# One pair of tiles instead of two multiplied block by block, in a conditional layer with a LoRA feed-forward (fp32, one core)

## The chip, the cores and the metric

The kernel runs on one core of a Trainium2 chip. The metric is device time in microseconds of one execution. Before the change the median of three runs is 460.17 us (460.08 to 460.25).

## The reference

x has 64 batches of 64 channels of 1024 values, so 4096 rows (tokens) of 1024. Each batch picks one of 16 matrices of 64x64, the rows are mixed with it, and the result goes through a linear layer with a gated low-rank addition:

```
W = weights[condition]                                  # [64, 64, 64]
y = einsum('bct,bcd->bdt', x, W)
gate_logits = einsum('bsd,ed->bse', y, gate_w)          # 8 experts
weights, selected = top_k(gate_logits, 2);  weights = softmax(weights)
result = einsum('bsd,od->bso', y, base_w) + base_b      # 1024 -> 1024
low = einsum('bsd,erd->ebsr', y, lora_A)                # rank 16
lora_out = einsum('ebsr,eor,bse->bso', low, lora_B, w_full)
out = x + result + 2.0 * lora_out
```

## The kernel before, in words

**Tiles.** The 4096 rows are 32 tiles of 128, taken as 16 pairs. The mixing matrix acts on rows and the linear layer on columns, so the kernel multiplies x by the big matrix first (z = x B) and mixes rows of z afterwards. B has 1024 rows and 1160 columns: 128 of the low-rank part, 8 of the gate, 1024 of the base weights, padded to three column groups of W = 388 (the first uses 384). With four groups of 256 rows, B is a 4x3 matrix of blocks b11 to b43, and a pair of tiles is a 2x4 matrix of blocks a11 to a24.

**High and low halves.** Every operand is split in two parts, high and low, and each product of two operands takes three matmuls: high x high, high x low, low x high. `split_x` (L280) does it for x blocks and `split_w` (L328) for weight blocks: ScalarE casts the high part (`copy`, L234), VectorE subtracts it to get the low part (`sub`, L231). `zstep` (L407, matmuls at L414) issues the three matmuls for one half f of a block of 256 rows, so a block product is six matmuls.

**Two ways to multiply a pair.** The plain way multiplies all 2 x 4 x 3 = 24 block pairs: 144 matmuls (`plain`, L612). The other way is a bilinear scheme with 20 products p1 to p20 (`class Pair`), 120 matmuls. It needs sums of x blocks (`Operands`, VectorE at L292), sums of weight blocks (`SUMS` and `make`, VectorE at L342, each then split like a block), and additions of the products from PSUM into SBUF (`mix`, VectorE at L740; `keep` and `pass_on`, ScalarE at L234 and L723). The sums of weights are made once and serve every later pair.

NPLAIN = 2 says how many pairs go the plain way. The list PLAIN (L539) holds their block steps, the first pair's with the order of the weights' loading, the later ones tile after tile. ORDER (L549) holds the products of the remaining pairs: the first HEAD, then for each pair its TAIL (p14, p15, p2, p8, p9) interleaved with the HEAD of the next.

**After z.** `post` (L508) takes a column group of a tile: zh and zl are split from it, L447 multiplies by the tile's mixing matrix (bdh, bdl), `gate` (L472) takes two of eight experts with small VectorE and ScalarE operations (the last at L493), L500 transposes the gated low part, its halves lth and ltl are split and multiplied by lbh and lbl. `finish` (L452) copies the outcome to xtok with ScalarE for tiles of plain pairs; for the others VectorE adds it to xtok at L457. For plain pairs x and the bias are added afterwards by accumulating DMAs on POOL (`late_sum`), for the others they are loaded and accumulated beforehand (`load_tok`, SP and POOL).

**What sets the order.** The body does not issue instructions directly. It adds steps to a `Program` (L80), each with an engine, a cost, what it reads and writes, and a due time. `run` (L111) then plans the steps on a model of the engines and issues them in the planned order, the one with the least slack first. The due times come from PLAIN and ORDER, and `ends[NPLAIN]` is the due time by which the sums of weights in SUMS and LATER are planned:

```
        pr.horizon, h = ends[NPLAIN], pr.horizon
        make(SUMS.get(m, ""))
        pr.horizon = h
```

On the chip every engine runs its instructions strictly in the issued order and waits on semaphores for the others. Matmul accumulators are eight PSUM banks: z0 to z3 (called X, Y, R, Q in the products), a0, a1, o0, o1. A product that reuses a bank waits until the earlier sum has been read from it.

Of the kernel before, what the change touches and what calls it, by code (L numbers as in the profile page):

```python
# [34 lines left out]
OUTS = ((NG, N0, 0), (0, W, N0 - NG), (0, W, N0 - NG + W))  # L35
KQ = 4
NPAIR = NT // 2
NPLAIN = 2
TOP = 3.0e38
NWARM = 39  # L40

# [38 lines left out]
class Program:  # L80
# [7 lines left out]
    def add(self, engine, cost, fn, reads=(), writes=(), due=None, first=False, size=0.0, early=None, port=False,  # L88
            after=0.0):

        n = len(self.steps)
        engine, cost = (e if isinstance(e, (list, tuple)) else [e] for e in (engine, cost))
        deps = set()
        for b in list(reads) + list(writes):
            if b in self.writer:
                deps.add(self.writer[b])
        for b in writes:
            deps.update(self.readers.get(b, ()))  # L100
        for b in reads:
            self.readers.setdefault(b, []).append(n)
        for b in writes:
            self.writer[b], self.readers[b] = n, []
        deps.discard(n)
        self.steps.append(dict(eng=dict(zip(engine, cost)), fn=fn, deps=deps, first=first, size=size, port=port,
                               lag=FLIGHT + QUEUE + size * DMA if size else 0.0, after=after,
                               due=self.horizon if due is None else due,
                               early=SP in engine and not reads if early is None else early))
# [59 lines left out]
def cond_ffn_kernel(ctx, tc, xT, x, idx, cw, wall, bias, lb, out):  # L169
# [63 lines left out]
    def copy(e, o, a):  # L233
        (nc.scalar.copy if e == ACT else nc.vector.tensor_copy)(o, a)  # L234
# [93 lines left out]
    def split_w(m, p, step=2):  # L328

        b, h, l = raw[m], Block(f"wh_{m}_{p}", F32R), Block(f"wl_{m}_{p}", F32R)  # L330
        hi[p], lo[p] = h, l
        for j in range(0, 2, step):
            a = slice(j, j + step)
            add(ACT, 0.2 + 0.00083 * W * step, lambda e, a=a: copy(e, h.ap()[:, a], b.ap()[:, a]), b.keys[a], h.keys[a])
            add(DVE, tt_cost(W * step), lambda e, a=a: sub(e, l.ap()[:, a], b.ap()[:, a], h.ap()[:, a]),
                b.keys[a] + h.keys[a], l.keys[a], port=True)
# [27 lines left out]
    def make(text):  # L364
        for q in (t.split() for t in text.split("; ") if t):
            if q[0] == "-":
                drop(raw.pop(q[1]))
            elif q[1] == ">":
                split_w(q[0], q[2])
                drop(raw.pop(q[0]))  # L370
            else:
                mix_w(q[0], q[2], q[4], ALU.add if q[3] == "+" else ALU.subtract, q[6] if len(q) > 5 else None)
# [55 lines left out]
    def outs(c):  # L428

        c, p = c if isinstance(c, tuple) else (c, slice(0, CN[c]))  # L430
        lo, o, n = max(OUTS[c][0] - p.start, 0), OUTS[c][2] + max(p.start - OUTS[c][0], 0), p.stop - p.start
        return n, slice(lo, n), slice(o, o + n - lo), p
# [19 lines left out]
    def finish(i, c, b):  # L452
        (_, s, o, _), j = outs(c), i % 3
        if i < 2 * NPLAIN:
            return add(ACT, 0.2 + 0.00085 * (s.stop - s.start), lambda e: copy(e, xtok[j][:, o], bank[b][:, s]),
# [84 lines left out]
    PLAIN += [(i, 2, k) for i in range(2) for k in LASTK]  # L540
    for q in range(1, NPLAIN):
        PLAIN += [(i, c, k) for c in range(3) for i in (2 * q, 2 * q + 1) for k in range(KQ)]
    t = 4.9
    for i, c, k in PLAIN:
# [3 lines left out]
        ends_plain = t  # L548
    ORDER = [(NPLAIN, p) for p in HEAD]  # L549
    for q in range(NPLAIN, NPAIR):  # L550
        if q == NPAIR - 2:
# [17 lines left out]
    def load_split_w(m, **how):  # L569
        load_w(m)  # L570
        split_w(m, SINGLE.get(m, m), **how)
        pr.horizon, h = ends[NPLAIN], pr.horizon
        make(SUMS.get(m, ""))
# [38 lines left out]
    def plain(i, c, k):  # L612
        if (i, k) not in xa0:
            us = xrs.two()
            for d in range(2):
                load_x(i, k + d, us[d])
            xa0[i, k], xa0[i, k + 1] = split_x(us)
            xrs.give(*us)
        if (i, c) not in zb:
            zb[i, c] = f"z{take('z', 4)}"  # L620
            if c == 0 and i > 1:
                load_cond(i)
        ks, m = LASTK if c == 2 and i < 2 else range(KQ), f"b{k + 1}{c + 1}"
        for f in range(2):
            zstep(("plain", i, c, k, f), zb[i, c], xa0[i, k], SINGLE.get(m, m), f, k == ks[0] and f == 0,
                  k == ks[-1] and f == 1, CN[c])
        left[i, k] -= 1
        if not left[i, k]:
            xas.give(xa0[i, k])
        if k == ks[-1]:  # L630
            post(i, c, split_z(CN[c], lambda: bank[zb[i, c]][:, :CN[c]], zb[i, c]))
            if c == 2:
                late_sum(i)
                store(i, range(3))

    for i, c, k in PLAIN:
        pr.horizon = due["plain", i, c, k, 1] + LAG + 8.0
        plain(i, c, k)
    pr.horizon = ends[NPLAIN]
    for m in ("b11", "b21", "b12", "b22", "b13", "b23", "b43"):  # L640
# [223 lines left out]
```

## Time and profile before

| what | value |
|---|---|
| median of 3 runs | 460.17 us (460.08 to 460.25) |
| the profiled execution | 460.46 us |
| its span, first to last instruction | 458.7 us |
| mean granted TensorE clock | 1.000 |
| ScalarE busy (ACT) | 227.2 us (50%) |
| VectorE subtractions for the low parts of x (L231, 512 wide) | 130, 685 ns each |
| VectorE additions of products (L740, 388 wide) | 126 with one PSUM operand first, 558 ns each |
| DMA | 75.00 MB, mean 164 GB/s |

PE is TensorE's matmuls and PEld its weight loads, DVE is VectorE, ACT ScalarE, POOL GpSimd and SP the queue that issues most loads. A duration in the profile is that of one instruction from its start to its end; successive instructions of an engine can overlap, so where an engine is full the distance between starts is shorter than the duration. In the rows of 40 slices one slice is 11.5 us. The first matmul on data starts at 5.02 us, the last result is added at 454.1 us.

### The profile page before, as it was taken

How to read it: one execution, taken by the hardware profiler on the slowest of the kernel's cores; microseconds unless marked ns; L12 is line 12 of the kernel's file. 1: busy time of each engine (PE TensorE's matmuls, PEld its weight loads, DVE VectorE, ACT ScalarE, POOL GpSimd, SP SyncE). 2: the span in 40 equal slices, each digit the busy share in tenths (PEclk: the TensorE clock that was granted, in tenths of full speed). 3: DMA queues.
4: the chain of work that ended last, by engine and by line, in shares of the span. 5: the costliest groups of instructions: out<-in, count | busy, mean ns of one | idle time of the engine just before them, and what ended most of it. 6: DMA issues, size and time to landing. Idle time of an engine off the chain costs nothing.

```text
span 458.7 us, 7577 instructions
## 1 busy us (share of the span) xinstructions
PE 452.7 (99%) x2621; PEld 449.7 (98%) x2621; DVE 383.5 (84%) x941; ACT 227.2 (50%) x520; POOL 89.6 (20%) x107
## 2 busy tenths in 40 slices
PE   8999999999999999999999999999999999999995
PEld 8999999999999999999999999999999999999995
DVE  5999997879989788796987979789797988888674
ACT  5864666543736345373543646354454544546331
POOL 3030214121303021220303003030210403103000
PEclk9999999999999999999999999999999999999999
DMA  8932748977768462764847456565565746556142
GB/s 279 352 117 47 153 107 198 213 211 202 180 206 202 172 161 87 217 131 163 199 127 202 108 182 148 172 162 133 191 123 185 173 129 193 116 174 149 51 134 91
DMA packets 36229, 75.00 MB, mean 164 GB/s; under 512 B 4432, under 2 KB 22240, under 8 KB 36192
## 3 DMA queue, kind: packets, MB, share of 16 engines
q0 software_dynamic: 10560, 36.72, 33.5%
q1 hardware_dynamic: 25200, 37.32, 25.9%
q10 hardware_dynamic: 432, 0.49, 0.4%
q8 instruction: 20, 0.33, 0.3%
q14 instruction: 17, 0.14, 0.1%
HBM read 57.74 MB, written 16.78 MB: 162 GB/s over the span
## 4 chain that ended last, share of the span: by engine, by line
PE 97%; DMA 1%; DVE 1%; ACT 0%; issue 0%
PE ps_z L414 76%; PE ps_o L447 15%; PE ps_a L447 6%; DMA w_b<-in_w 1%; PE ps_a L500 1%; DVE wl_b_b L231 0%; DVE xtok L457 0%; DVE st L740 0%; ACT wh_b_b L234 0%; DVE xl L231 0%; PE ps_z L447 0%; DVE xh L234 0%
## 5 line engine op out<-in xcount | busy, mean ns | idle before, releaser
L231 DVE TENSOR_TENSOR xl<-xr,xh 128x512 fp32r<-128x512 f32 (+1 forms) x138 | 92.1, 670 | 20.0 <-ACT xh L234 19.8
L414 PE MATMUL ps_z<-wh_t_p,xh 128*128 128x388 f32 (+1 forms) x308 | 105.3, 342 | 0.1
L414 PE MATMUL ps_z<-wh_t_p,xl 128*128 128x388 f32 (+1 forms) x308 | 104.3, 339 | 0.0
L414 PE MATMUL ps_z<-wl_t_p,xh 128*128 128x388 f32 (+1 forms) x308 | 104.3, 339 | 0.0
L234 ACT CAST xh<-xr 128x512 fp32r<-128x512 f32 (+1 forms) x136 | 82.5, 610 | 37.2 <-PE ps_z L414 32.5
L740 DVE TENSOR_TENSOR st<-ps_z,st 128x388 f32<-128x388 f32 x126 | 70.2, 558 | 21.2 <-PE ps_z L414 20.2
L292 DVE TENSOR_TENSOR xr<-xr 128x256 f32<-128x256 f32 (+1 forms) x139 | 69.6, 526 | 3.6 <-DMA xr<-in_xT 3.4
L414 PE MATMUL ps_z<-wh_b_p,xh 128*128 128x388 f32 (+1 forms) x180 | 61.4, 341 | 0.0
L414 PE MATMUL ps_z<-wh_b_p,xl 128*128 128x388 f32 (+1 forms) x180 | 60.9, 338 | 0.0
L414 PE MATMUL ps_z<-wl_b_p,xh 128*128 128x388 f32 (+1 forms) x180 | 60.8, 338 | 0.0
L414 PEld LDWEIGHTS ps_z<-wh_t_p,xh 128*128 128x128 f32 x308 | 57.8, 188 | 1.2 <-DVE st L740 0.7
L414 PEld LDWEIGHTS ps_z<-wl_t_p,xh 128*128 128x128 f32 x308 | 57.9, 188 | 0.0
L414 PEld LDWEIGHTS ps_z<-wh_t_p,xl 128*128 128x128 f32 x308 | 57.9, 188 | 0.0
L464 POOL DMA_DIRECT2D out<-xtok x30 | 16.8, 560 | 193.6 <-DVE xtok L457 89.6
L234 ACT CAST zh<-st 128x388 fp32r<-128x388 f32 (+1 forms) x70 | 36.1, 517 | 22.1 <-DVE st L740 15.2
L381 POOL DMA_DIRECT2D xtok<-in_bias x28 | 27.0, 964 | 96.9 <-DMA xtok<-in_x 89.6
L394 POOL DMA_INDIRECT bdr<-in_cw,rows x32 | 36.9, 1155 | 26.4 <-DVE zl L231 17.7
L457 DVE TENSOR_TENSOR xtok<-ps_o,xtok 128x388 f32<-128x388 f32 (+1 forms) x56 | 30.9, 554 | 11.2 <-PE ps_o L447 10.7
L723 ACT ACTIVATE ps_z<-ps_z 128x388 f32<-128x388 f32 x42 | 20.1, 478 | 40.5 <-PE ps_z L414 39.4
L231 DVE TENSOR_TENSOR zl<-st,zh 128x388 fp32r<-128x388 f32 (+1 forms) x70 | 38.7, 554 | 0.9 <-ACT zh L234 0.6
L414 PEld LDWEIGHTS ps_z<-wh_b_p,xh 128*128 128x128 f32 x180 | 33.8, 188 | 0.2
L414 PEld LDWEIGHTS ps_z<-wl_b_p,xh 128*128 128x128 f32 x180 | 33.8, 188 | 0.0
(143 smaller groups left out, 873.0 us busy)
## 6 DMA issues: line engine op xcount, KB each, us to landing
xr<-in_xT SPq DMA_DIRECT2D x128, 128.0 KB, 3.2
xtok<-in_bias POOLq DMA_DIRECT2D x32, 512.0 KB, 7.1
out<-xtok POOLq DMA_DIRECT2D x30, 512.0 KB, 3.2
xtok<-in_x SPq DMA_DIRECT2D x28, 512.0 KB, 3.6
w_b<-in_w SPq DMA_DIRECT2D x10, 388.0 KB, 5.9
xtok<-in_x POOLq DMA_DIRECT2D x4, 512.0 KB, 6.6
out<-xtok SPq DMA_DIRECT2D x3, 194.0 KB, 2.2
bdr<-in_cw,rows POOLq DMA_INDIRECT x32, 5.3
```

The costliest lines, as they stand in the source:

```text
L231: eng[e].tensor_tensor(o, a, b.bitcast(F32), ALU.subtract)
L234: (nc.scalar.copy if e == ACT else nc.vector.tensor_copy)(o, a)
L292: add(DVE, tt_cost(2 * P * len(os)), lambda e: nc.vector.tensor_tensor(some(xr, os), some(xr, xs), some(xr, ys), f), [("xr", u) for u in s ...
L381: add(POOL, 1.1, lambda e: nc.gpsimd.dma_start(xtok[j], bias.broadcast_to([P, T]), accum_op=ALU.add), writes=keys, size=TWICE * 4.0 * T * P)
L394: add(POOL, 1.04, lambda e: nc.gpsimd.indirect_dma_start(out=bdr[j], out_offset=None, in_=cw, in_offset=bass.IndirectOffsetOnAxis(ap=rows[ ...
L414: nc.tensor.matmul(z, l[:, j, n], w.ap()[:, f, :cols], start=(start and q == 0), stop=(stop and q == 2), skip_group_check=True)
L447: nc.tensor.matmul(d, l, r, start=(start and m == 0), stop=(stop and m == len(mms) - 1), skip_group_check=True)
L457: add(DVE, 0.09 + 0.00104 * (s.stop - s.start), lambda e: nc.vector.tensor_tensor(xtok[j][:, o], bank[b][:, s], xtok[j][:, o], ALU.add), [ ...
L464: add(POOL, 1.0, lambda e: nc.gpsimd.dma_start(out[i * P:(i + 1) * P, o], xtok[j][:, o]), src, size=4.0 * P * (o.stop - o.start))
L500: add(PE, 0.107, lambda e: nc.tensor.matmul(tp, low[i % 2][:, :ER], ident, is_transpose=True, start=False, stop=False, skip_group_check=True),
L723: add(ACT, 0.2 + 0.00085 * W, lambda e: nc.scalar.mul(z[b], z[x], scale), [BANKS[x]], [BANKS[b]])
L740: add(DVE, 0.09 + 0.00104 * W, lambda e: nc.vector.tensor_tensor(unit(u), a(), b(), f), reads, [ukey(u)])
```

## The change

One constant is changed.

```diff
@@ -35,7 +35,7 @@
 OUTS = ((NG, N0, 0), (0, W, N0 - NG), (0, W, N0 - NG + W))
 KQ = 4
 NPAIR = NT // 2
-NPLAIN = 2
+NPLAIN = 1
 TOP = 3.0e38
 NWARM = 39
```

With it PLAIN holds the steps of pair 0 only, and ORDER begins with the twenty products of pair 1, whose x sums, additions of products and token loads go the way of the other pairs. The due time of the sums of weights, `ends[NPLAIN]`, becomes the end of pair 1's products instead of pair 2's. In `finish`, tiles 2 and 3 are added by VectorE instead of being copied by ScalarE. The planner plans all steps anew, so the order of instructions on every engine changes from the first microseconds on.

## The prediction

> **What bounds the kernel now.** I read the page's busy shares first, then busy time by stage, the chain that ended last, the waits, and the timeline of the first 75 us.
>
> ```profile
> PE 452.7 (99%) x2621; PEld 449.7 (98%) x2621; DVE 383.5 (84%) x941; ACT 227.2 (50%) x520; POOL 89.6 (20%) x107
> ...
> PE   8999999999999999999999999999999999999995
> ...
> DVE  5999997879989788796987979789797988888674
> ...
> PEclk9999999999999999999999999999999999999999
> ...
> PE 97%; DMA 1%; DVE 1%; ACT 0%; issue 0%
> ```
>
> Over the span TensorE is the bound: both its rows are full, the clock is whole, the chain is 97% matmuls. But VectorE's row stands at 9 in slices 2 to 6, so I cut the span by stage.
>
> ```profile
> core 0: us, PE busy (x) PEld busy (x) DVE busy (x) ACT busy (x) POOL busy (x), PEclk, DMA share, GB/s
> 9.00:75.00 66.00, 66.00 (x380) 65.56 (x379) 63.16 (x121) 43.51 (x90) 12.33 (x13) 1.00 0.60 168
> 75.00:102.00 27.00, 27.00 (x158) 26.96 (x157) 21.84 (x55) 13.65 (x33) 6.97 (x9) 1.00 0.87 201
> 102.00:129.00 27.00, 27.00 (x158) 26.92 (x157) 24.16 (x63) 13.14 (x31) 6.01 (x7) 1.00 0.77 205
> 129.00:156.00 27.00, 27.00 (x156) 26.93 (x156) 23.82 (x63) 12.90 (x32) 5.66 (x7) 1.00 0.62 184
> ```
>
> From 9 to 75 us two engines are full at once: TensorE 66.0 of 66, VectorE 63.2 of 66. VectorE splits the weights there and builds their sums. Afterwards it needs 21.8 to 24.2 us of each 27.0 (one pair of tiles, 158 matmuls). The only margin in the first stage is that the weight sums are wanted late:
>
> ```profile
> 72.81 0.96 DVE L231 TENSOR_TENSOR wl_g_p<-w_b,wh_g_p 128x776 fp32r<-128x776 f32 x1
> ...
> 96.64 0.33 PE L414 MATMUL ps_z<-wl_g_p,xh 128*128 128x388 f32 x1
> ```
>
> The last weight operand (wl_g, for p9) is ready at 73.8 and first used at 96.64: 22.8 us of lead. TensorE's waits hold 1.7 us on VectorE in all.
>
> **Matmuls removed.** The order in which the two programs queue their instructions differs by 24 matmuls, all 384 columns wide at L414. Consecutive starts of such matmuls are 0.175 us apart (10.23 to 10.40), so 24 x 0.175 = 4.2 us off TensorE. If TensorE stays the bound, all of it counts.
>
> Here a rule speaks for the change. The Trainium skill, Perfetto Trace Analysis, section Identifying the Most-Contended Engine, says to optimize the engine with the highest occupancy, TensorE judged by its weight-load share: 98% against VectorE's 84%. By it the sum is 460.46 - 4.2 = 456.3. The row of 9 to 75 us has the matmuls leave just where VectorE is at 96%, so the shares over the span don't settle it.
>
> **Work added to VectorE.** Counted in both orders, with the spacing of consecutive starts (776 wide 0.876, 512 0.603, 388 0.475, 256 0.335, 248 0.32): 15 more of 512 (9.0), 14 more of 388 (6.7), 2 more of 248 (0.6), 6 fewer of 256 (-2.0). That is 14.3 us more over the kernel. After 75 us VectorE has about 3 us to spare per pair, so there it costs nothing; before 75 us nothing hides it. ScalarE gains five 512-wide casts (0.62 each) and three copies (0.48) and loses three smaller ones, about 3 us; at 43.5 of 66 it has room, so I cost that at nothing. If ScalarE's queue failed to keep ahead, its casts would delay VectorE one for one, which the idle term below covers.
>
> **Weight sums moved.** All 20 products' weights are now wanted one pair earlier, so the 22.8 us lead meets a TensorE that arrives some 34 us sooner. VectorE queues its work in order, so I add up its queue in the changed program from the b21 split (9.04 us, the same place as before) to the wl_g split: 44 of 776 (38.5), 15 of 512 (9.0), 17 of 388 or 384 (8.1), 16 of 256 (5.4), 6 of 128 (1.2), lbl (1.14), small gate operations (2.1): 65.5 us, so wl_g is ready at 74.5 at the earliest. The same sum over the old queue gives 71.7 against 73.8 seen, so it errs low by about 2.
>
> TensorE, also in order, reaches the matmul reading wl_g after 309 matmuls from the one at 8.10. In the trace 508 matmuls from that one took 88.54 us (to 96.64), or 0.1743 each: 62.0. So it waits 74.5 - 62.0 = 12.5 us at least. Other points in the same two queues:
>
> The transpose of tile 1's gate wants L493's output at 34.9; the VectorE queue gives it at 40.3: 5.4 late. p18's xl half: wanted 46.4, ready 59.2: 12.8. p10 of the first product pair writes the bank that L740 must first read for c12: wanted 51.3, free 64.9: 13.6. p10 of the next pair: wanted 78.9 (406 matmuls), free 92.8: 13.9. Beyond that VectorE gains its 3 us per pair, and I count no more waits. These are waits of one in-order queue on another, so the largest counts, not their sum: 13.9 us if VectorE never idles.
>
> It idles some. A weight sum waits for nothing new, but behind L740, L486 and the ltl split (each waits for TensorE or ScalarE) the whole VectorE queue stands, the xl halves included, and TensorE stands for those. From both sides: 0 at least; at most 2.8, the idle time of the 9 to 75 row. I take 1.2, because 1.1 of that 2.8 was one wait at 73.8 to 74.9, by which time VectorE had caught up, and part lies ahead of work that nobody needed yet. Total wait 15.1.
>
> A second rule bears on the 65.5. The Trainium skill, VectorE: DVE Perf Modes, section The TRN2 errata, gives (N+151)/0.96 ns for an fp32 two-input operation: 966 for 776. The row shows 0.96 as duration, but starts 0.876 apart (12.43 and 13.31 for 776 wide): the end of one overlaps the next. Summing durations would add about 0.088 for each of the 92 large instructions, 8.1 us, and give some 479; I take the spacing.
>
> **Queues and loads.** The x tiles for the second pair's products are loaded by SP from about 20 us, ahead of and around b23; the row's DMA share of 0.60 and a landing time of 3.2 us leave room. POOL's accumulations for tile 2 move ahead of bdr loads needed only near 73 us. Nothing, at least nothing below zero since TensorE isn't fed sooner; at most one landing, 3.2, inside the range.
>
> **Sum.** Profiled execution 460.46 (span 458.7 and 1.8 around it) - 4.2 + 15.1 = 471.4. The median of the runs is 0.3 below that execution: 471.1.
>
> **Rivals.**
> First, the gain holds: faster, 460.17 - 4.2 = 456.0. Its one mechanism is that TensorE's wait stays below 4.2 us, because the sums needed for each product are always built ahead. It decides at p10: VectorE would have to deliver by 51.3 + 4.2 = 55.5 what its queue ends at 64.9, so 46.5 us for 55.9 us of work. For it: 22.8 us of lead, no wait over 0.4 us now. Against: the queue is in order and VectorE was full. 4%.
> Second, only the wl_g point binds (VectorE runs gapless and later banks come free sooner): 460.17 - 4.2 + 12.5 = 468.5. 18%.
> Third, hand-offs between the two engines add to the queue: both starved engines wait on each other at each of the c22, c12, c13 sums, the idle term is 2.8 and a load adds up to 3.2: 472.7 to about 476. 22%.
> My forecast, 469.5 to 472.7: 54%. The gain and the wait cancel (460): 2%; I know no reason for it but chance. That the change doesn't do what it says is excluded by the 24 matmuls counted.
>
> A measurement tells about 0.2% of this kernel from no change: faster 0.04, within 0.01, slower 0.95. The range takes in the second case and half of the third: 468.3 to 475.
>
> **What would show it.** TensorE idle of about 15 us between 34 and 95 us, put down to VectorE (first at the L500 transpose near 35 us, then xl and wl of the second pair, then L740); VectorE near 100% from 9 to 75; no new idle after 100 us; wl_g's split ending near 75 to 76. If TensorE's gaps are under 8 us or continue into every later pair, or if ScalarE or a DMA ends them, my sum is wrong.

## The result, and the profile after

The changed kernel takes 479.91 us (median of 479.85, 479.88, 479.95 and 485.0) against 460.21 for the kernel before beside it: a ratio of 1.0453, 95% interval 1.0402 to 1.0504. That is 19.7 us slower, 8.8 more than forecast, and above the range (468.3 to 475.0). The profiled execution is one of 479.85 us, with a span of 478.1.

The page of the changed kernel, same rows as before the change:

```profile
PE 455.2 (95%) x2597; PEld 446.7 (93%) x2597; DVE 398.1 (83%) x966; ACT 229.2 (48%) x525; POOL 87.8 (18%) x105
...
PE   8894989999999999999989999999999999999996
...
DVE  4899999998698878979877888988788897877675
...
PEclk9898899999999999999999999999999999999999
...
PE 80%; DVE 10%; DMA 7%; issue 2%; ACT 1%; POOL 0%; DVEq 0%; POOLq 0%; ACTq 0%
```

The counted edits are there: 24 matmuls fewer (2621 to 2597), and VectorE has 25 instructions and 14.6 us of busy time more (383.5 to 398.1; 14.3 was counted). What differs is the chain: TensorE's share has fallen from 97% to 80%, VectorE holds 10%, and DMA holds 7%, which no step of the prediction had. In TensorE's row, slices 2, 4 (36 to 48 us) and 6 are no longer full, nor is slice 21, near 245 us. Busy time by stage, in the stages used before:

```profile
core 0: us, PE busy (x) PEld busy (x) DVE busy (x) ACT busy (x) POOL busy (x), PEclk, DMA share, GB/s
9.00:75.00 66.00, 53.85 (x275) 50.30 (x274) 61.76 (x107) 38.84 (x75) 10.13 (x12) 0.92 0.65 179
75.00:102.00 27.00, 26.36 (x152) 25.75 (x151) 25.85 (x67) 12.35 (x32) 6.73 (x7) 1.00 0.55 164
102.00:129.00 27.00, 26.44 (x153) 26.06 (x152) 22.03 (x55) 12.61 (x31) 5.74 (x6) 1.00 0.65 169
129.00:156.00 27.00, 25.85 (x150) 25.44 (x149) 22.47 (x58) 12.30 (x30) 5.01 (x6) 1.00 0.51 139
```

From 9 to 75 us TensorE gets 275 matmuls through instead of 380. That was forecast in kind. Two things were not: VectorE is busy 61.8 of 66, so it idles for 4.2 us in a stage where I had allowed 1.2; and after 102 us, with VectorE at 22 of 27 and so with time to spare, TensorE still issues 149 to 152 weight loads where it issued 156 or 157. The waits of TensorE's weight loads over the whole kernel (us in total, times, longest):

```profile
PEld ps_z L414 <- DVE st L740: 6.5, 7, 2.1
PEld ps_z L414 <- DVE xl L231: 4.5, 4, 2.7
PEld ps_a L500 <- DVE low L493: 4.3, 1, 4.3
PEld ps_z L414 <- ACT xh L234: 2.8, 1, 2.8
```

Before, all waits on VectorE behind 5 us summed to 1.7 and none was on ScalarE. Beside VectorE's queue, which was forecast, two of these lines led to causes that were not.

**A wait on ScalarE, at 11 us.** The timelines of TensorE, ScalarE and VectorE of the changed kernel, in order of time (start, duration; the bracket is idle time before the instruction and what ended it):

```profile
12.42 0.30 ACT L234 CAST bdh<-bdr 128x128 fp32r<-128x128 f32 x1 [3.12 <-DMA bdr<-in_cw,rows]
...
12.75 0.29 DVE L231 TENSOR_TENSOR bdl<-bdr,bdh 128x128 fp32r<-128x128 f32 x1 [2.43 <-ACT bdh L234]
...
13.82 0.45 PE L414 MATMUL ps_z<-wh_b_b,xh 128*128 128x384 f32 x1 [2.47 <-ACT xh L234]
```

The replanned ScalarE queue has the cast of the first gathered mixing matrix (bdh) right behind the casts that start at 8.15 and 8.90. The gather was issued on POOL at 6.67 and has landed about 5.7 us later, so ScalarE stands still from 9.3 to 12.4, its next casts of weights and x stand behind it, VectorE behind those, and TensorE behind both. In the kernel before, the same cast lay eight casts further back, and found its data there:

```profile
15.12 0.29 ACT L234 CAST bdh<-bdr 128x128 fp32r<-128x128 f32 x1
```

**Waits on L740 behind a load.** 5.4 of the 6.5 us of the first line lie after 105 us (before: 0.7). One of them, in the timelines of POOL, SP, VectorE and TensorE:

```profile
233.90 1.03 POOL L381 DMA_DIRECT2D xtok<-in_bias  x1
...
234.47 0.33 SPq L380 DMA_DIRECT2D xtok<-in_x  x1
235.23 0.33 SPq L276 DMA_DIRECT2D xr<-in_xT  x1
...
241.57 0.69 DVE L292 TENSOR_TENSOR xr<-xr 128x512 f32<-128x512 f32 x1 [2.29 <-DMA xr<-in_xT]
...
243.00 0.55 DVE L740 TENSOR_TENSOR st<-ps_z,st 128x388 f32<-128x388 f32 x1
...
243.60 0.44 PE L414 MATMUL ps_z<-wh_h_p,xh 128*128 128x388 f32 x1 [1.77 <-DVE st L740]
```

An x load, issued just behind a bias accumulation and a token load, needs 6.3 us (235.23 to 241.57, when the instruction that waits for it starts) where the page's median is 3.0. VectorE's sum of x blocks (L292) waits for it at the head of the queue, the addition L740 that frees a PSUM bank stands behind it, and TensorE waits for the bank. L292 waits 10.1 us for x loads after 105 us, ten times. Before the change, in the same window:

```profile
DVE xr L292 <- DMA xr<-in_xT: 0.8, 2, 0.5
PEld ps_z L414 <- DVE st L740: 0.7, 2, 0.4
```

To place the loss I add up TensorE's lateness: the sum of what the distance between two successive matmul starts exceeds the usual one (0.176 us for 388 columns, 0.175 for 384, 0.115 for 248), from 5 us on. This is worked out from the timelines; the labels of the experiments stand in the section below.

| lateness of TensorE up to | 50 us | 103.5 us | 200 us | 440 us |
|---|---|---|---|---|
| before | 1.6 | 2.2 | 2.9 | 5.2 |
| after | 14.5 | 21.7 | 24.1 | 29.1 |
| bd | 12.6 | 19.1 | 21.6 | 25.2 |
| bdthinx | 12.0 | 17.7 | 19.1 | 22.0 |
| bdthinb | 11.2 | 17.3 | 18.2 | 20.6 |
| bdlo | 11.4 | 11.9 | 12.8 | 15.3 |
| bdlo2 | 11.5 | 15.6 | 17.3 | 27.7 |

After minus before is 19.5 us up to 103.5 us and 4.4 behind that. With the 4.2 us of matmuls that are gone, 23.9 - 4.2 = 19.7, against 19.4 between the two profiled executions.

### The profile page after: what moved, and what is told of

Read it like the earlier page. It is cut to its first block, busy times and chain, and to the rows that moved or that the text cites. A ratio compares the mean times of both kernels' runs of the same rounds, so it can differ in the third digit from the quotient of the medians.

```text
span 478.1 us, 7584 instructions
## 1 busy us (share of the span) xinstructions
PE 455.2 (95%) x2597; PEld 446.7 (93%) x2597; DVE 398.1 (83%) x966; ACT 229.2 (48%) x525; POOL 87.8 (18%) x105
## 4 chain that ended last, share of the span: by engine, by line
PE 80%; DVE 10%; DMA 7%; issue 2%; ACT 1%; POOL 0%; DVEq 0%; POOLq 0%; ACTq 0%
PE ps_z L414 61%; PE ps_o L447 13%; PE ps_a L447 5%; DMA xr<-in_xT 4%; DVE xl L231 2%; DVE xr L292 2%; DVE wl_t_p L231 1%; DVE st L740 1%; DMA bdr<-in_cw,rows 1%; DVE w_b L342 1%; DVE zl L231 1%; DMA idx_sb<-in_idx 1%; PE ps_a L500 1%; DVE xtok L457 1%; ACT xh L234 1%
## 5 line engine op out<-in xcount | busy, mean ns | idle before, releaser
L414 PE MATMUL ps_z<-wh_t_p,xh 128*128 128x388 f32 (+1 forms) x330 | 113.3, 343 | 1.6 <-ACT ps_z L723 1.4
L414 PE MATMUL ps_z<-wl_t_p,xh 128*128 128x388 f32 (+1 forms) x330 | 112.0, 339 | 0.8 <-DVE wl_t_p L231 0.8
L414 PE MATMUL ps_z<-wh_t_p,xl 128*128 128x388 f32 (+1 forms) x330 | 111.9, 339 | 0.5 <-DVE xl L231 0.5
L231 DVE TENSOR_TENSOR xl<-xr,xh 128x512 fp32r<-128x512 f32 (+1 forms) x143 | 95.7, 671 | 19.6 <-ACT xh L234 19.1
L740 DVE TENSOR_TENSOR st<-ps_z,st 128x388 f32<-128x388 f32 x135 | 75.0, 557 | 13.8 <-PE ps_z L414 13.0
L292 DVE TENSOR_TENSOR xr<-xr 128x512 f32<-128x512 f32 (+1 forms) x143 | 75.1, 543 | 11.0 <-DMA xr<-in_xT 10.7
L414 PEld LDWEIGHTS ps_z<-wh_t_p,xh 128*128 128x128 f32 x330 | 62.2, 188 | 3.9 <-ACT ps_z L723 2.1
L414 PEld LDWEIGHTS ps_z<-wl_t_p,xh 128*128 128x128 f32 x330 | 62.2, 189 | 1.1 <-DVE wl_t_p L231 1.1
L414 PEld LDWEIGHTS ps_z<-wh_t_p,xl 128*128 128x128 f32 x330 | 62.2, 188 | 1.1 <-DVE xl L231 1.1
L381 POOL DMA_DIRECT2D xtok<-in_bias x30 | 28.4, 947 | 79.2 <-DMA xtok<-in_x 70.4
L234 ACT CAST bdh<-bdr 128x128 fp32r<-128x128 f32 x32 | 9.5, 300 | 61.0 <-PE ps_o L447 57.9
```

Of the source, the lines that this page charges most:

```text
L231: eng[e].tensor_tensor(o, a, b.bitcast(F32), ALU.subtract)
L292: add(DVE, tt_cost(2 * P * len(os)), lambda e: nc.vector.tensor_tensor(some(xr, os), some(xr, xs), some(xr, ys), f), [("xr", u) for u in s ...
L381: add(POOL, 1.1, lambda e: nc.gpsimd.dma_start(xtok[j], bias.broadcast_to([P, T]), accum_op=ALU.add), writes=keys, size=TWICE * 4.0 * T * P)
L414: nc.tensor.matmul(z, l[:, j, n], w.ap()[:, f, :cols], start=(start and q == 0), stop=(stop and q == 2), skip_group_check=True)
L740: add(DVE, 0.09 + 0.00104 * W, lambda e: nc.vector.tensor_tensor(unit(u), a(), b(), f), reads, [ukey(u)])
```

## The experiments

The theory after the result: three waits, one behind the other. VectorE's queue up to the last weight sum (the forecast, some 15 us), the gather's cast in ScalarE's queue (some 3 to 4), and x loads that land late after 100 us (some 4 to 5). Rivals: the whole loss is VectorE's queue, and the other two waits hide in it; or TensorE's clock, which fell to 0.5 of full speed behind the long waits, is part of it.

**bd: the changed kernel, with the gather's cast planned no earlier than 16 us.**

```diff
-        add(ACT, 0.28, lambda e: copy(e, bdh[j], bdr[j]), [("bdr", j)], [("bdh", j)])
+        add(ACT, 0.28, lambda e: copy(e, bdh[j], bdr[j]), [("bdr", j)], [("bdh", j)], after=16.0)
```

> The changed kernel with one thing put back: ScalarE's cast of the first two gathered mixing matrices (bdh) may be planned no earlier than 16 us, so that it no longer stands in ScalarE's queue ahead of the casts of b22 and of x blocks while its gather is still on its way. Theory of an early queue block (3.1 us of ScalarE waiting for the gather, passed on to VectorE and from there through its full queue to every later product): 476.3 to 477 us, 3 to 3.6 below the changed kernel's 479.9. Rival, that VectorE's later backlog hides that wait (largest wait counts, not the sum): 479 to 480, no change.

Measured: 476.11 us, ratio 1.0342 (1.0325 to 1.036): 3.8 us less than the changed kernel. The cast now starts at 16.82 without a wait. So the standstill was not hidden behind VectorE's shortage: it comes first in time, and all three engines stand in it. By the lateness, 2.6 of it come back before 103.5 us and 1.3 behind it, where the new plan of the whole kernel also lies a little otherwise. All further experiments but n3 start from bd.

**bdlo: bd, and the low halves of the last ten weight sums are not computed** (their matmuls read the high half instead; that part of the products is left out).

```diff
+HALF = ("p10", "p4", "p13", "p7", "p17", "p3", "p15", "p14", "p8", "p9")
...
-        b, h, l = raw[m], Block(f"wh_{m}_{p}", F32R), Block(f"wl_{m}_{p}", F32R)
+        b, h = raw[m], Block(f"wh_{m}_{p}", F32R)
+        l = h if p in HALF else Block(f"wl_{m}_{p}", F32R)
...
+            if l is h:
+                continue
```

> As bd, and VectorE no longer computes the low halves of ten weight sums (those of p10, p4, p13, p7, p17, p3, p15, p14, p8, p9): the matmuls that read them read the high half instead, so the number of matmuls is the same and that part of the result is left out. It takes 10 x 0.876 = 8.8 us out of VectorE's queue before 80 us. Theory that VectorE's queue of weight work sets the first 75 us: 7 to 9 us below bd, about 468. Rival, that hand-offs and a lowered TensorE clock set it: under 3 us below bd.

Measured: 466.15, ratio 1.0125 (1.0108 to 1.0142): 10.0 us less than bd for ten instructions of 0.876 us, 8.8 us of VectorE's queue. By the lateness 7.2 come back up to 103.5 us (19.1 to 11.9) and 2.7 later. 6.0 of the 7.2 lie between 50 and 103.5 us. bd by stage, with the columns as above:

```profile
50.00:75.00 25.00, 22.46 (x120) 20.58 (x119) 24.07 (x46) 14.89 (x31) 4.94 (x6) 1.00 0.76 192
```

and bdlo:

```profile
50.00:75.00 25.00, 25.00 (x144) 24.97 (x143) 23.84 (x60) 17.31 (x38) 6.39 (x7) 1.00 0.75 200
75.00:102.00 27.00, 27.00 (x158) 26.93 (x157) 24.26 (x62) 12.06 (x29) 5.89 (x7) 1.00 0.66 183
```

VectorE is about as full as in bd, but finishes the sums sooner, and TensorE is full again from 50 us on. So VectorE's queue sets the stretch from 50 us to its last weight sum. Ahead of 50 us bdlo gives nothing back: its lateness there is 11.4, bdthinb, which keeps all the sums, has 11.2, and the two first long waits are as in bd (4.5 us at the transpose of tile 1, 2.4 at the xl half behind it). What puts these down to VectorE's queue is bd's trace:

```profile
30.00:41.00 11.00, 6.59 (x38) 6.03 (x37) 11.00 (x22) 7.93 (x16) 3.13 (x3) 0.95 0.08 11
```

VectorE has no idle time in the 11 us that end with the first of the two waits, while TensorE is busy for 6.6 of them (11.0 of 11 in the kernel before). No run took work out of VectorE's queue ahead of 41 us and nothing else: of the 16.9 us that bd loses up to 103.5 us, some 6 are shown by bdlo and some 11 are read from the trace.

**bdlo2: the same for the last two sums only**, `HALF = ("p8", "p9")`, behind the point p10.

> bd without the low halves of the last two weight sums, those of p8 and p9 (their matmuls read the high half in its place; that part of the product is left out). 1.75 us less of VectorE's queue, but only behind the point p10 of the first product pair. Theory A (one in-order queue waits on another, the largest wait counts, and the largest are the ones at p10 and before): little comes back before p10; what comes back is what the points behind it still wait, 474.5 to 476. Rival B (VectorE is simply full to its last weight sum, so each us taken from it anywhere before 79 us comes back in full): 476.1 - 1.75 = 474.3 or less, 474.4 at most.

Measured: 478.1 (476.42 to 481.31), ratio 1.039 (1.0339 to 1.0442), slower than bd if anything. Neither case. The edit makes the planner lay out the whole kernel anew: up to 103.5 us the lateness is 15.6 (3.5 less than bd, more than either said), and behind that 12.1 come (bd 6.1), with L740 waiting 8.7 us after 105 us. The run can't tell the two apart, and it shows how far the late waits move with a plan that was not meant to touch them.

**bdtok: bd, and POOL instead of SP issues the token loads**, so that no x load stands behind one in SP's queue.

```diff
-        add(SP, ISSUE, lambda e: nc.sync.dma_start(xtok[j], x[i * P:(i + 1) * P, :]), writes=keys, size=4.0 * T * P)
+        add(POOL, 1.1, lambda e: nc.gpsimd.dma_start(xtok[j], x[i * P:(i + 1) * P, :]), writes=keys, size=4.0 * T * P,
+            early=True)
```

> As bd, and the loads of x for the residual (load_tok) are issued by POOL instead of SP, so that the x blocks' loads on SP no longer queue behind loads that wait for a store. Theory that the waits after 100 us (four of 0.7 to 1.9 us, p15 behind L740 behind an L292 that waits for its x load) come from SP's queue: 4 to 5 us below bd, about 472. Rivals: POOL's own queue holds the loads up and VectorE waits for xtok instead (no gain or slower); or the planner puts L292 too early whatever the queue (no change).

Measured: 473.67, ratio 1.029 (1.0273 to 1.0307), 2.4 less than bd, but L292 still waits 7.8 us for x loads after 105 us (bd 7.2), and the plan of the first 45 us is another one. So the place behind the token load in SP's queue is not what delays the x loads.

**bdnobias: bd without the accumulation of the bias for tiles 2 to 31** (the bias is left out there).

```diff
-        add(POOL, 1.1, lambda e: nc.gpsimd.dma_start(xtok[j], bias.broadcast_to([P, T]), accum_op=ALU.add),
-            writes=keys, size=TWICE * 4.0 * T * P)
```

> As bd, without the accumulating DMAs of the bias for tiles 2 to 31 (that part of the result is left out); it removes 15 MB of traffic and 30 steps from POOL's queue. Theory that the waits after 100 us are x loads delayed by token loads and bias accumulations on the same wires: DMA waits of L292 fall from 7.2 to under 3 us, TensorE's waits at p15 disappear, 472.5 to 474 (3 below bd). Rival, that the x loads are issued too late because their buffers come free too late: as bd, 475.5 to 476.5.

Measured: 469.79, ratio 1.0203 (1.0186 to 1.022), 6.3 less than bd. L292 waits 1.5 us for x loads. The late waits hang on this traffic; but the plan changed again, and about 3.3 of the 6.3 lie before 103.5 us.

**bdthinx and bdthinb: bd with every instruction in its place, and only the bytes taken away.** From tile 5 on the token load (bdthinx) or the bias accumulation (bdthinb) moves 8 columns instead of 1024; the rest of x or of the bias is left out for those tiles.

```diff
-        add(SP, ISSUE, lambda e: nc.sync.dma_start(xtok[j], x[i * P:(i + 1) * P, :]), writes=keys, size=4.0 * T * P)
+        add(SP, ISSUE, lambda e: nc.sync.dma_start(xtok[j][:, :(T if i < 5 else 8)], x[i * P:(i + 1) * P, :(T if i < 5 else 8)]), writes=keys, size=4.0 * T * P)
```

> bd with every instruction in its place, but from tile 5 on the token load brings 8 columns instead of 1024 (so most of x is not added for those tiles: left out). It asks which bytes delay the x loads that VectorE's first sum of a pair (L292) waits for after 105 us: 7.2 us in bd, and about 3 us of TensorE's idle time behind that. Theory 1 (the x load stands behind the 512 KB token load in SP's queue, issued 0.4 us earlier): L292 waits under 3 us, landing of those x loads under 4 us, about 473. Theory 2 (the bias accumulation, which reads and writes at the same time, takes the bandwidth): little change, 475.3 to 476.3. Theory 3 (simply the sum of the bytes in flight): half, 474 to 475, and the same from thinning the bias.

> bd with every instruction in its place, but from tile 5 on the bias is accumulated on 8 columns instead of 1024 (the rest of the bias is left out for those tiles). Theory 1 (token load in SP's queue): no change, 475.3 to 476.3, L292 still waits 6 to 8 us for x. Theory 2 (bias traffic): L292 waits under 3 us, about 473, and no gap of TensorE at L740 ahead of p15 after 105 us. Theory 3 (sum of bytes): 474 to 475. In each, the waits before 103 us should stay as in bd, since the order of instructions is the same; the 6.3 us that leaving the bias out altogether brought were partly another plan of the first 45 us.

Measured: bdthinx 472.61, ratio 1.0265 (1.0248 to 1.0282); bdthinb 472.45, ratio 1.0269 (1.025 to 1.0288). Each is about 3.6 us less than bd. Neither the first theory nor the second holds, which left one of the two without effect. The waits of L292 after 105 us, in bd:

```profile
DVE xr L292 <- DMA xr<-in_xT: 7.2, 9, 1.8
```

in bdthinx:

```profile
DVE xr L292 <- DMA xr<-in_xT: 4.9, 8, 1.0
```

and in bdthinb:

```profile
DVE xr L292 <- DMA xr<-in_xT: 3.9, 7, 1.0
```

The longest wait falls from 1.8 to 1.0 us whichever transfer is thinned, and TensorE's waits on L740 after 105 us fall from 3.9 in bd to 2.1 and 1.0. By the lateness behind 103.5 us, bd has 6.1, bdthinx 4.3, bdthinb 3.3, and the kernel before had 3.0. So the x loads are late because both transfers are under way, as in the third theory (which had put the time at 474 to 475), the bias with the larger part. But this is 1.8 and 2.8 us, not 3.6: the other 1.4 to 1.8 stand before 103.5 us, most of it before 70 us, where the three kernels do the same (the first thinned load is issued at 92.6 us in bd). One profile of the same order differs from another by that much in the early stretch, and the medians of runs on two chips can't separate it.

**bdwarm: bd, and TensorE does 38 and 20 small matmuls of 124 columns on spare columns of a bank in its two long waits** (before the transpose of tile 1 and before the first xl half of p6).

```diff
+    def fill(n):
+        for _ in range(n):
+            nc.tensor.matmul(bank["o1"][:, W:], lbh[:, :P], lbh[:, :512 - W], start=True, stop=True,
+                             skip_group_check=True)
...
+                if key == (NPLAIN, "p6", 0) and q == 2:
+                    fill(20)
```

> As bd, with 38 idle matmuls of 124 columns ahead of the transpose of tile 1's gate and 20 ahead of p6's first use of its low x half, in the places where TensorE waits in bd (4.3 and 2.2 us); they write columns of a bank that nobody reads. Their purpose is to keep the granted clock up, which in bd and in the changed kernel falls to 0.5 to 0.75 after those waits. Theory that VectorE's queue sets this stretch and TensorE arrives early at every later point even with half its clock: clock near 1.0 from 40 to 55 us, time as bd, 475.5 to 476.5. Rival, that the lowered clock is itself part of the loss (in bd matmuls from 44 to 54 us take about 3.4 us more than at full clock): 472.5 to 473.5.

Measured: 475.99 (475.0 to 479.4, five runs), ratio 1.0335 (1.0314 to 1.0356), the same as bd. The profile is of the longest of the five, 479.4; what it has more than bd lies behind 103.5 us. The stage of the long waits in bd:

```profile
40.00:44.00 4.00, 1.22 (x4) 0.71 (x4) 4.00 (x8) 1.70 (x4) 2.35 (x2) 0.50 0.86 146
44.00:48.00 4.00, 4.00 (x14) 4.00 (x15) 4.00 (x7) 1.30 (x2) 0.92 (x1) 0.50 1.04 207
48.00:52.00 4.00, 4.00 (x19) 4.00 (x19) 3.67 (x6) 2.88 (x8) 0.00 (x0) 0.74 0.32 62
```

and in bdwarm, where the small matmuls are counted in the first row:

```profile
40.00:44.00 4.00, 3.84 (x30) 3.56 (x30) 4.00 (x8) 1.37 (x3) 2.02 (x2) 1.00 0.98 169
44.00:48.00 4.00, 4.00 (x26) 4.00 (x25) 4.00 (x7) 2.63 (x5) 0.92 (x1) 1.00 1.05 213
48.00:52.00 4.00, 3.21 (x15) 2.09 (x13) 4.00 (x7) 3.16 (x9) 1.44 (x2) 1.00 0.39 55
```

The granted clock (the column after POOL's) is whole throughout, 26 matmuls instead of 14 go through from 44 to 48 us, and then TensorE waits again at 48 to 52: VectorE (the third pair of numbers) is full in bdwarm and nearly so in bd. The rule in the Trainium skill, TensorE: Matmul & The Clock Gate, section Why this matters for your kernels, to avoid idle gaps of over some 3 us in TensorE, has its trigger here (a wait of 4.2 us and a clock of 0.50 behind it). What it would save by the clock (some 2 us from 44 to 48 us alone, an estimate from 14 matmuls, most of them at 0.325 us instead of 0.175) did not show in the runs, since another engine sets the pace there. The clock rival in its size, some 3 us, falls; a share of about 1 us can't be told, because profiles with bd's order differ by as much (wl_g's split ends at 76.5 in bd, 75.2 in bdthinb, 75.1 in bdwarm).

Where TensorE sets the pace, the low clock does cost time. In the same profile of bdwarm one of the late waits on the addition of products (L740 before the edit), 2.6 us and so shorter than the some 3 us of that rule, ends at 129.3, and behind it:

```profile
130.00:134.00 4.00, 4.00 (x16) 4.00 (x15) 2.91 (x13) 1.56 (x6) 0.00 (x0) 0.57 0.02 4
134.00:138.00 4.00, 4.00 (x24) 3.96 (x24) 2.90 (x9) 3.25 (x8) 0.00 (x0) 1.00 0.11 34
```

That is 16 matmuls instead of 24, some 1.5 us (an estimate: ten at 0.325 us instead of 0.175), on top of the wait itself. In the profile of the changed kernel the late waits are shorter (1.8 us at 243.6) and the clock stays at 1.00 behind them, so this is no part of its 19.7.

**bdpool: bd, and the planner may give the weight sums (L342) to POOL.**

```diff
-        add(DVE, tt_cost(2 * W), lambda e: nc.vector.tensor_tensor(r.ap(), x.ap(), y.ap(), f),
-            [k for z in (x, y) if z is not r for k in z.keys], r.keys, port=True, after=FIRST)
+        add((DVE, POOL), (tt_cost(2 * W), 1.8), lambda e: eng[e].tensor_tensor(r.ap(), x.ap(), y.ap(), f),
+            [k for z in (x, y) if z is not r for k in z.keys], r.keys, after=FIRST)
```

> As bd, and the planner may put a sum of weights on POOL instead of VectorE, which it does for 13 of the 20. If POOL's sums run beside VectorE's instructions, VectorE's queue is 13 x 0.876 = 11.4 us shorter before 75 us and the time falls by 8 to 11, to about 466. If the two exclude each other or a sum on POOL takes over 2 us, POOL's chain of sums becomes what TensorE waits for: as bd or slower, 476 to 490.

Measured: 478.6, ratio 1.0391 (1.0374 to 1.0409), 2.5 slower than bd, although 13 of the 20 sums left VectorE's queue. The reason is in the section on the hardware below.

**n3: the kernel before with a third plain pair**, `NPLAIN = 3`: the change the other way.

> The kernel before with NPLAIN = 3: the third pair is multiplied block by block too. Theory that TensorE is the bound where VectorE has its lead: 24 matmuls of 0.175 more, 464.3 to 464.5. Rival, that replanning brings or removes waits of its own (as after 100 us in the changed kernel): more than 1 us off that.

Measured: 466.32 (465.16 to 467.28), ratio 1.0132 (1.0106 to 1.0159), 6.1 us more than the kernel before, 5.3 by the profiled execution, where 4.2 was expected: the rival, over 1 us off, came. VectorE falls to 49.1 of 66 us from 9 to 75 and TensorE stays at 65.8: no VectorE work that this pair takes away was on the path. Up to 440 us TensorE's lateness is that of the kernel before; behind that come two new waits on ScalarE, 1.1 us (zh) and 0.9 (lth). So 24 matmuls cost 4.2 us when TensorE is full, and the rest of the profile's 5.3 is the new plan's end. The 0.8 by which the median exceeds the profile was not traced.

## Why the prediction was wrong

The forecast was 471.1 and the result 479.9. By TensorE's lateness against the kernel before: 16.9 us up to 103.5 us in bd (VectorE's queue), 2.6 more there in the changed kernel (the cast), 4.4 behind that point (late x loads), less 4.2 for the matmuls: 19.7. By the medians the cast is 3.8.

- **Matmuls removed, 4.2 us.** Right: 24 are gone, and n3 shows the price from the other side.
- **The rule of the most-contended engine (456.3).** The decision against it was right: over the span TensorE is still first (PEld 93%, VectorE 83%), and the kernel is slower although TensorE has less to do.
- **Work added to VectorE, 14.3 us.** Right: 14.6 in the busy time.
- **"At 43.5 of 66 it has room, so I cost that at nothing" (ScalarE).** This step failed. ScalarE is busy only 38.8 of 66 us after the change, and yet its queue cost 2.6 to 3.8 us: an in-order queue with room still stops when its next instruction waits for a DMA. I counted how many casts were added, and did not look at which cast had moved past which, though the order of ScalarE's instructions was in view, and the gather's issue time (6.87) and its median landing (5.3 us) stood in the profile of before: together about 12.2, while the cast now stood right behind one that starts at 8.9. I had written that ScalarE's casts would delay VectorE one for one if its queue failed to keep ahead, and left this to the idle term of 1.2; VectorE idled 4.2 in the stage, 2.4 of it in this one wait.
- **Weight sums moved, 13.9 + 1.2 = 15.1 us.** Right in mechanism and nearly in size: up to 103.5 us bd is 16.9 above the kernel before, bdthinx 15.5 and bdthinb 15.1, with one order of instructions. bdlo shows the queue as the cause from 50 us on, the trace ahead of that. The spacing of starts was the right measure: in bd, where ScalarE does not stand still, wl_g's split ends at 76.5, where the sum gave 74.5, or 75.7 with the idle term, and a sum of durations would have given 82.6. That the sum of durations, some 479 for the whole kernel, is near the measured 479.9 is chance: two waits that it does not contain fill the difference. The points came in the order given: the transpose of tile 1 (5.4 forecast, 4.3 measured), the xl half of the second pair, then the sums and their banks. In the changed kernel itself wl_g's split ended at 79.2, not 75 to 76; in bdthinb at 75.2.
- **"Beyond that VectorE gains 3 us per pair, and I count no more waits", and "Nothing" for queues and loads.** This failed too, by 4.4 us. VectorE did have its spare time (22 of 27 us per pair), but spare time on average doesn't help an in-order queue that meets a load landing 2 us late. I looked for loads in the first 75 us only. Which pairs it strikes depends on the new plan, in which x loads fall together with a token load and a bias accumulation of 512 KB each. bdthinb, with 3.3 us behind 103.5 us, is nearly back at the 3.0 of the kernel before: so much is shown for the 6.1 of bd, and the changed kernel's 7.4 contain 1.3 more that no run took away alone.
- **What would make it wrong** named both signs: gaps that go on into every later pair, and gaps ended by ScalarE or a DMA. Both came, the first in some of the later pairs. The third rival, hand-offs and a load, had the right kind of addition, but put it at one landing and before 95 us.

Open: how much of the late waits is bound to this plan. bdlo2, with two VectorE instructions fewer, has 12.1 us of lateness after 103.5 us, bd 6.1, the kernel before 3.0; why the one plan brings x loads and other transfers together more often was not traced. And of the 3.8 us between bd and the changed kernel, 1.3 lie behind 103.5 us: part of what I count to the cast may be late waits of another plan, and profiles with bd's order differ by 1.4 to 1.8 us ahead of it. The late waits also differ between executions of one kernel: one of bdwarm's five runs took 479.4, its late waits being longer than bd's, where the other four lie between 475.0 and 476.5. One of the changed kernel's four took 485.0, where the others lie within 0.1 us of 479.9; of that one there is no profile.

## What to carry to other kernels

When a planner lays the instructions out anew, compare the order of every in-order queue, idle ones too, and ask of each instruction that moved forward whether its data has landed by then: the slack of an engine says nothing about that. An engine that has lost its lead pays for every late load that it used to cover, so cost a lost lead for the whole kernel and not only for the stage in which it is lost. To test a suspected transfer, take away its bytes and leave every instruction in place; edits that let the planner start over moved other waits by up to 6 us here.

## What the hardware showed that I had not expected

**VectorE and POOL shut each other out.** bdpool's timelines of POOL and VectorE:

```profile
12.40 2.07 POOL L342 TENSOR_TENSOR w_t<-w_u,w_b 128x776 f32<-128x776 f32 x1 [0.78 <-DMA w_b<-in_w]
...
16.59 1.98 POOL L342 TENSOR_TENSOR w_b<-w_b,w_b 128x776 f32<-128x776 f32 x1 [2.12 <-DMA w_b<-in_w]
...
12.70 2.06 DVE L231 TENSOR_TENSOR xl<-xr,xh 128x256 fp32r<-128x256 f32 x1
...
16.76 2.63 DVE L231 TENSOR_TENSOR wl_b_p<-w_b,wh_b_p 128x776 fp32r<-128x776 f32 x1
...
23.03 0.41 DVE L231 TENSOR_TENSOR xl<-xr,xh 128x256 fp32r<-128x256 f32 x1
```

A subtraction of 256 columns that takes 0.41 us alone (at 23.03, with no sum on POOL) takes 2.06 beside a sum on POOL, and ends when that sum has ended (14.76 after 14.47); one of 776 takes 2.63 instead of 0.96. This is the exclusive lock that the Trainium skill describes (SBUF — State Buffer, section SBUF: two separate sides: the loser blocks for the whole instruction), for a VectorE instruction with two SBUF inputs against a POOL instruction that reads SBUF. A sum on POOL (2.39 us on average in the largest group of them) so can take over 2 us out of VectorE's queue instead of 0.876: from 9 to 44 us VectorE got 30 instructions through, in bd 62.

**An x load of 128 KB lands after 6.3 us instead of 3.0** when a token load and a bias accumulation of 512 KB each are under way, and taking the bytes of either away shortens the longest wait of L292 from 1.8 (bd) to 1.0 us. **TensorE's granted clock fell to 0.50** behind a wait of 4.2 us in bd and stayed there until about 50 us, at no cost that the runs show, because VectorE set the pace; behind a late wait of 2.6 us in bdwarm, where TensorE sets it, the same fall cost some 1.5 us.
